# A convolution, selective-scan and attention kernel: the head by lines with two PSUM tiles in turn, the first delta kept in SBUF, four lanes for the last stage

## The chip, the cores and the metric

The kernel runs on one core of one Trainium2 chip. The metric is the device time of one execution in microseconds (us); smaller is better. Times are medians of several executions, and every run counted here is of the fast state or, where a kernel ran only once, of a state that can't be told. Two executions of the same kernel easily differ by 10 us (26 runs of the kernel before lay between 5500.35 and 5524.82), so single microseconds are read from the profiles, as far as they repeat (see e0 to e2), and the times say whether they arrive at the end.

## The reference, cut to what matters

Four images of 64 x 64 pixels and 96 channels pass one convolution block with a selective scan in four directions, then linear attention and a small feed-forward net.

```python
# per image: L = 4096 pixels, Dn = 192 channels, N = 16 states, K = 4 directions
xz = bilinear(groupnorm(x), W_in)            # products of signs
xp, z = split(xz)
t = conv3x3(sign(xp + move0), sc * sign(conv_W)) + biases
t = prelu(t) + xp
u = t * sigmoid(t)                           # silu
xs = [u by rows, u by columns, both backwards]
dts, B, C = bilinear(xs, Wl)                 # again products of signs
delta = softplus(bilinear(dts, Wd) + bias)
h = exp(delta * A) * h + (delta * u) * B     # the scan along the 4096 pixels
y = sum_over_states(h * C) + D * u
out = layernorm(sum of the 4 directions) * silu(z) @ W_out   # then + x
t = t + linear_attention(layernorm(t)); t = t + ffn(layernorm(t))
```

The names in the profile follow this: `cv` is the convolution's result in PSUM, `v` and `r` are the two branches of prelu, `u` the block's result and `ut` the same by columns, `xg` and `sg` its signs, `xr` the signs transposed, `tbc` the rows of B and C, `gT` the signs that delta is made from, `dl` delta and delta * u spread over the 16 states, `bc` B and C spread over the channels.

## The kernel before

The scan is cut into 1536 pieces of 128 x 1024. For each piece GpSimd makes the input w = (delta u) * B, ScalarE the decay, VectorE the scan, and the product with C goes to VectorE or GpSimd, whichever a running tally of costs finds less loaded:

```python
lead = c.vec.us - c.gps.us
c.vec.us, c.gps.us = max(0.0, min(lead, 8.0)), max(0.0, min(-lead, 8.0))
pool = c.vec.us + 1.2 > c.gps.us + 2.4          # the product goes to GpSimd
h = c.p.h.tile([128, CH], F32, ...) if pool else dA
c.vec.tensor_tensor_scan(h, dA, w, first, ALU.mult, ALU.add)
```

The head (image 0 alone, nothing of the scans beside it) loads small weights early, makes the convolution part by part in the two halves of one PSUM tile, and starts the scans by way of memory:

```python
for g in range(NG):                              # 24 loads of 2 KB each
    ...
        nc.sync.dma_start(anm[j::4, g, :], src[j])
...
two = [c.p.dA.tile([128, CH], F32, ...) for i in range(2)] if alone else None
parts = [(h, q) for h in range(2) for q in range(NQ8)]
for n, part in enumerate(parts + [None]):
    at = 512 * (n % 2)
    ps = two[0][:, at : at + 512]                # 15 groups of matmuls into ps
    ...
    nc.vector.tensor_scalar(v, ps, ...)
    nc.scalar.activation(r, ps, AF.Relu, ...)
...
def run(self, back):
    ...                                          # three parts of delta, stored to dld
    c.later.flush()
    self.load_dl(0)                              # and loaded again, spread over the states
    for m in (1, 2):
        self.load_dl(m)
    ...                                          # a fourth part before the loop
    self.decay(0)
    for i in range(AHEAD):
        self.inject(i)                           # w of the first four pieces, GpSimd
    for i in range(n): ...                       # loop: inject(i + 4), product of i - 1, scan(i)
```

The tail is the last image's layer norms ("sums"), one small step ("middle") and the last stage ("last"), in three lanes that step in turn:

```python
e.alone = True
more = [e.spare_lane(x) for x in range(2)]
drain([behind] + [e.sums(ln) for ln in more])
drain([e.middle()])
drain([e.last(ln) for ln in [e.lane] + more])
```

## Time and profile before

| kernel before | |
|---|---|
| median of the first 3 runs | 5511.64 us (5508.68 to 5516.53) |
| span of the profiled execution (its time 5505.96 us) | 5504.2 us |
| convolution starts | 71.2 us |
| last u | 192.7 us |
| gT complete | 231.1 us |
| GpSimd's first product for the scans | 260.93 us |
| last product of the scans ends | 5388.80 us |
| from there to the end | 115.4 us |

The times inside are read from the list of instructions of the profiled execution, counted from its start. The profiled execution was one of the quick ones of its kernel; a second profile of the same head (e2) has the last u 5 us earlier. The lines of the profile that carry the argument stand in the prediction.

### The profile page before, as it was taken

What the parts mean: (1) busy time and instruction counts of PE and PEld (TensorE: products, weight loads), DVE (VectorE), ACT (ScalarE), POOL (GpSimd) and SP (SyncE); (2) the same over time, 40 slices, a digit from 0 to 9 for tenths busy, and PEclk for the clock granted to TensorE, in tenths of its full rate; (3) what the DMA queues carried; (4) which work ended last, traced back from release to release, by engine and by line L of the source; (5) the groups of instructions that cost most, each with busy time, mean ns of one, the idle gap of its engine ahead of it and who ended that gap; (6) DMA issues with size and microseconds to landing.
All of it is one profiled execution on the core that took longest, in us unless ns stands there. A gap on an engine that the chain in (4) does not pass through costs nothing. (4 is left out here: it accounts for less than half of the span.)

```text
span 5504.2 us, 62064 instructions
## 1 busy us (share of the span) xinstructions
PE 3466.0 (63%) x20089; PEld 1360.3 (25%) x20089; DVE 4996.1 (91%) x3142; ACT 3631.0 (66%) x5673; POOL 4947.3 (90%) x2247
## 2 busy tenths in 40 slices
PE   5456765467655776656665677664777664444677
PEld 2221222122222232222222222221232221111223
DVE  3299999999999999999999999999999999999884
ACT  4468776677766667777767666775656775655544
POOL 2199999899999999999999999999999999999981
PEclk7666876578867777768876787766787665556777
DMA  4455665766666666676765666666666565765642
GB/s 78 122 184 195 206 203 188 245 214 208 209 200 202 195 205 211 201 235 212 219 192 185 207 211 195 205 217 225 198 209 203 178 198 196 219 204 185 203 152 60
DMA packets 613659, 1069.84 MB, mean 194 GB/s; under 512 B 225147, under 2 KB 344468, under 8 KB 611540
## 3 DMA queue, kind: packets, MB, share of 16 engines
q1 hardware_dynamic: 612244, 1065.86, 61.3%
q8 instruction: 157, 2.57, 0.2%
q14 instruction: 170, 1.39, 0.1%
q10 hardware_dynamic: 1088, 0.02, 0.0%
HBM read 833.16 MB, written 229.35 MB: 193 GB/s over the span
## 5 line engine op out<-in xcount | busy, mean ns | idle before, releaser
L421 POOL TENSOR_TENSOR w<-dl,bc 128x1024 f32<-128x1024 f32 x1536 | 3580.9, 2358 | 155.5 <-PE yp L1409 72.6
L1336 ACT ACTIVATE dA<-dl,anm 128x1024 f32<-128x1024 f32 x1536 | 1714.5, 1116 | 474.4 <-DVE w L421 285.8
L421 DVE TENSOR_TENSOR_SCAN dA<-dA,cy,w 128x1024 f32<-128x1024 f32 x726 | 1700.9, 2343 | 90.7 <-ACT dA L1336 75.5
L1409 PE MATMUL yp<-w,sum 128*32 128x256 f32 x12288 | 1286.6, 514 | 384.8 <-POOL w L421 230.7
L421 POOL TENSOR_TENSOR w<-h,bc 128x1024 f32<-128x1024 f32 x573 | 1349.1, 2355 | 124.1 <-DVE h L421 110.0
L421 DVE TENSOR_TENSOR w<-dA,bc 128x1024 f32<-128x1024 f32 x963 | 1179.5, 1225 | 54.7 <-DVE dA L421 0.5
L421 DVE TENSOR_TENSOR_SCAN h<-dA,cy,w 128x1024 f32<-128x1024 f32 x426 | 996.7, 2340 | 16.0 <-ACT dA L1336 15.8
L1409 PEld LDWEIGHTS yp<-w,sum 128*32 128x32 f32 x12288 | 315.6, 128 | 1467.9 <-issue 690.1
L1378 ACT COPY cy<-dA 128x1 f32<-128x1 f32 x721 | 113.5, 157 | 772.5 <-DVE w L421 770.6
L421 DVE TENSOR_TENSOR_SCAN dA<-dA,w 128x1024 f32<-128x1024 f32 x237 | 540.9, 2282 | 36.7 <-ACT dA L1336 28.4
L1271 PE MATMUL dps<-gT,wdz 128*128 128x64 fp8e5 x1000 | 113.9, 313 | 358.8 <-ACT ys L1423 329.8
L421 DVE TENSOR_TENSOR_SCAN h<-dA,w 128x1024 f32<-128x1024 f32 x147 | 334.8, 2278 | 4.9 <-ACT dA L1336 3.4
L1284 PE MATMUL dps<-sp,ident 128*128 128x512 f32 x376 | 273.0, 815 | 46.0 <-ACT dps L1280 45.8
L1414 PE MATMUL yp<-ya,back 128*128 128x256 f32 x576 | 235.1, 528 | 4.5 <-DMA ya<-yd 2.5
L659 PE MATMUL cv<-tp,cwA 128*96 128x512 fp8e5 x576 | 198.4, 470 | 60.3 <-ACT r L706 55.1
L1271 PEld LDWEIGHTS <-wdz 128*128 128x128 fp8e5 x1024 | 95.4, 152 | 440.1 <-issue 409.7
L1271 PE MATMUL dps<-gT,wdy 128*128 128x64 fp8e5 x504 | 58.5, 317 | 205.2 <-ACT ys L1423 203.2
L1276 ACT ACTIVATE pd<-dps,dbias,pvd 128x512 f32<-128x512 f32 x188 | 143.3, 762 | 20.2 <-PE dps L1271 20.2
L1414 PEld LDWEIGHTS yp<-ya,back 128*128 128x128 f32 x576 | 122.6, 246 | 133.4 <-issue 93.5
L1378 ACT COPY cy<-h 128x1 f32<-128x1 f32 x431 | 79.9, 185 | 113.7 <-DVE h L421 112.8
L941 PE MATMUL yc<-eys,mean 96*96 96x512 f32 x240 | 132.1, 702 | 24.2 <-DVE vks L421 8.9
L1277 ACT ACTIVATE sp<-dps,dbias,pvd 128x512 f32<-128x512 f32 x188 | 144.2, 767 | 0.0
(312 smaller groups left out, 4433.1 us busy)
## 6 DMA issues: line engine op xcount, KB each, us to landing
dl<-dld SPq DMA_DIRECT2D x768, 512.0 KB
bc<-bcd SPq DMA_DIRECT2D x512, 512.0 KB
dld<-pd SPq DMA_DIRECT2D x125, 512.0 KB
yd<-ys SPq DMA_DIRECT2D x768, 64.0 KB
dld<-pd SPq DMA_DIRECT2D x126, 256.0 KB
ya<-yd SPq DMA_DIRECT2D x192, 128.0 KB
pu<-ud SPq DMA_DIRECT2D x32, 512.0 KB
pu<-utd SPq DMA_DIRECT2D x30, 512.0 KB
```

What stands on the lines that cost most here:

```text
L421: return getattr(self.eng, name)(out, *args, **kw)
L659: nc.tensor.matmul(ps, w[:, 96 * h : 96 * h + 96], tp[:, 8 * q + dy : 8 * q + dy + 8, dx : dx + IW], start=(w is taps[0][1]), stop=(w is t ...
L941: self.c.nc.tensor.matmul(ps, w, x, start=(i == 0), stop=(i == len(pairs) - 1))
L1271: nc.tensor.matmul(pv[:, s], wd[:, k, s], gT[:, :, c0 : c0 + 16], start=(s == 0), stop=(s == 7))
L1276: nc.scalar.activation(d[:, 0], ps, AF.Abs, scale=sc, bias=bi)
L1277: nc.scalar.activation(t, ps, AF.Relu, scale=sc, bias=bi)
L1284: nc.tensor.matmul(ps, c.ident, t, start=False, stop=True, skip_group_check=True)
L1336: c.nc.scalar.activation(t, self.dlt[i // NQ][0], AF.Exp, scale=c.anm[:, g, NQ * KORD[e] + q : NQ * KORD[e] + q + 1])
L1378: self.c.nc.scalar.copy(self.carries[g, q], h[:, CH - 1 : CH])
L1409: c.nc.tensor.matmul(y[32 * x : 32 * x + 32, g % 2, :], c.sum4, prod[:, 256 * x : 256 * x + 256], start=(q == 0), stop=(q == NQ - 1 and no ...
L1414: c.nc.tensor.matmul(y[:, g % 2, :], w, src, start=False, stop=(n == len(more) - 1))
```

## The change

Its intent is to shorten what isn't scans. It loads the small weights last, alternates two PSUM tiles in the convolution and goes through it by lines (both halves of the channels of a line, then the next line), stores signs in larger pieces, makes the first delta out of SBUF and spreads it from SBUF to SBUF, and at the end uses four lanes and loads the short operands first. Cut to its core:

```diff
-        (early)  sbR and anm loads
+        (after all weights)
+        for k in range(NK):  nc.sync.dma_start(sbR[...], ...)            # 12 issues
+        for g in range(NG):  ... nc.sync.dma_start(anm[j::4, g, :], ...) # 24 issues
@@ projections
-                px, pz = two[1][:, 0:512], two[1][0:96, 512:CH]
+                px, pz = (c.p.ps.tile([128, 512], F32, ..., tag=f"y{j}") for j, x in enumerate("xz"))
-                sz = c.p.h.tile([128, CH], F32, ...)           # stored for each q
+                    if q % 4 == 0:
+                        szs[h] = c.p.w.tile([128, CH], F32, ...)  # stored for four q at once
@@ convolution
+                parts = [(h, q) for q in range(NQ8) for h in range(2)]
-                    ps = (two[0][:, at : at + 512] if alone else bank("cv" + nm, 0))[0:96]
+                        ps = c.p.dA.tile([128, CH], F32, name=f"cv{nm}_{b}", tag="dA")[0:96, 0:512]
+                per = 2 if alone and h else 4                   # u by columns: six stores for four
@@ transposes
+            xrs = rw.tile([128, 96, 64], BF16, ...)             # first in its pool
-                        nc.scalar.copy(prev[0], prev[1])
+                        (nc.vector.tensor_copy if fast and n % 2 else nc.scalar.copy)(prev[0], prev[1])
@@ scans
-        pool = c.vec.us + 1.2 > c.gps.us + 2.4
+        pool = c.vec.us + 1.2 > c.gps.us + 2.4 and i < len(self.pieces) - 2
+    def start(self):                                            # two parts of delta, then
+        for n in range(3):
+            for x in range(2):
+                r = p.dl.tile([128, CH], F32, ...)
+                nc.sync.dma_start(r, w[x][32 * n : 32 * n + 32].unsqueeze(1).to_broadcast([32, 4, CH]))
+            if n == 0:
+                for q in range(NQ):
+                    self.load_bc(1, self.ct, 0, 0, 0, q)
@@ tail
+    more.append(e.fourth_lane())                                # between middle and sums
-                self.loads(ln, q, ("ys", "sz", "xb"))
+                self.loads(ln, q, ("sz", "xb", "ys") if self.alone else ("ys", "sz", "xb"))
-        c.gps.tensor_tensor(m0, self.vks, c.hmask, ALU.mult)
+        (c.vec if self.alone else c.gps).tensor_tensor(m0, self.vks, c.hmask, ALU.mult)
```

## The prediction

> **What bounds the kernel now.** I read the page first: the span, the busy shares, the forty slices.
>
> ```profile
> span 5504.2 us, 62064 instructions
> PE 3466.0 (63%) x20089; PEld 1360.3 (25%) x20089; DVE 4996.1 (91%) x3142; ACT 3631.0 (66%) x5673; POOL 4947.3 (90%) x2247
> DVE  3299999999999999999999999999999999999884
> POOL 2199999899999999999999999999999999999981
> ```
>
> VectorE and GpSimd are both full from the third slice to the last but one. Then I cut the span with the stage table at the first scan work (GpSimd's first product starts at 260.9 us) and at the last product (5388.8 us).
>
> ```profile
> core 0: us, PE busy (x) PEld busy (x) DVE busy (x) ACT busy (x) POOL busy (x), PEclk, DMA share, GB/s
> 275.00:5389.00 5114.00, 3245.84 (x19162) 1246.97 (x19165) 4867.19 (x2907) 3446.53 (x5370) 4889.09 (x2130) 0.72 0.63 202
> ```
>
> In those 5114 us each of the two is busy 95%, and the diff alters two of the 1536 pieces there. So the change can only shorten the head (261 us) and the tail (5504 - 5389 = 115 us). All 376 us would have to shrink by 110 us to reach 2%. What the head waits for, from the waits of 56 to 200 us and of 203 to 280 us:
>
> ```profile
> PE cv L659 <- ACT r L706: 33.3, 15, 3.7
> POOL ut L634 <- DMA utd<-ut: 25.2, 3, 8.5
> ACT r L706 <- DVE v L703: 21.2, 11, 2.9
> ACT sz L600 <- DMA szd<-sz: 12.2, 1, 12.2
> ...
> POOL w L421 <- DMA dl<-dld: 57.8, 1, 57.8
> DVE w_s L421 <- DMA pu_s<-utd: 22.3, 1, 22.3
> ACT xr L740 <- DMA utd<-ut: 10.2, 1, 10.2
> ```
>
> First number: us in total. Line 1: each convolution part's matmuls wait until ScalarE has read the part before, though they go to the other half of the tile. Line 4: one stop of 12.2 us before the convolution. Its cause is in SyncE's timeline: the store of sz stands behind 18 us of issues for anm.
>
> ```profile
> 43.03 18.07 SPq L269 DMA_DIRECT2D anm<-in_al  x24
> 61.21 4.49 SPq L440 DMA_DIRECT2D xbd<-xb  x8
> 65.80 14.37 SPq L440 DMA_DIRECT2D szd<-sz  x6
> ```
>
> **What the Trainium skill says.** (1) "PSUM — Partial Sum Buffer", section "PSUM bank collisions raise a hardware error": two engines may not touch one bank and quadrant at once, reads included, and the compiler orders them. The trace agrees: r (ScalarE) and v (VectorE) only read the same tile, yet r starts 0.83 us after v, in 11 waits. (2) "DMA: Bandwidth & Descriptors", "Rules for kernel authors": a strided last dimension becomes one descriptor per element. The trace agrees: an anm load of 2 KB holds SyncE for 18.07 / 24 = 0.75 us. (3) Same page, "Anatomy of one DMA": about 2.0 us fixed per transfer. The trace has more in queues: 7.0 us from the first dl issue (253.90) to GpSimd's start (260.93). (4) "GPSIMD Engine Reference", "Elementwise — side-by-side cycle accounting": float32 tensor_tensor is 1.96 times slower there than on VectorE. Here 2355 against 1225 ns, 1.92.
>
> **The change part by part.**
>
> *Up to the convolution (starts 71.2 us now).* The new yield puts the column sums ahead of the w_in signs. Now the sums start at 18.60, behind ScalarE's twelve sbR issues and those signs; x is issued by 4.6 us, so they can run from about 5 to 13 us. The next barrier is older: VectorE reads cw_n until 25.6 us, since the loads land then; xb, now on VectorE, queues behind that, and GpSimd's sign copies follow. So the chain is ahead by some 4.5 us at 33 us (copies begin at 29 in place of 33.8), not by 13. Without the stop of 12.2 us the convolution would now begin near 58.5. Minus 4.5 gives 54. Against it: the projections move to banks y0 and y1, which the weights' transposes use, so casts (1.22 us) and signs (1.5 to 2.3 us) alternate with the matmuls; five such rounds at some 0.5 us each: start 56, a gain of **15**.
>
> *The convolution.* Two tiles end the wait of line 1, but another loop is hidden right behind it: v 0.84, r 0.82, second combination 0.8, sign 0.6, exponential 0.6, logarithm and exponential 1.3, u 0.7, then v again: 5.65 us, exactly the distance of parts that run undisturbed (v at 138.80 and 144.44). v and r still share a bank. Only the four parts that came 1.0 to 1.25 us late behind TensorE gain: about **5** with part 0. The twelve projections are the same ScalarE work, one per part in place of two: nothing. But anm (18 us) and sbR (twelve issues of about 0.4, some 5 us) now come in at the second part, in front of u's and sg's stores; v of part n reuses the buffer of sg of part n-2, sg that of u of part n-2. SyncE blocks from about 9 to 32 us after the start, part 2's sg was due at 22 and can run at 33: a loss of **12**. The by-columns stores become six in place of four, each holding the queue 6 us (the 6.03 after a utd issue), twice two in a row: a loss of **3**. In sum the convolution costs 10 more; its last u, now at 192.7, comes at about 187.7.
>
> *Transposes.* xr now lies first in its pool, so it no longer waits for the by-columns store (10.1 us from the last u to its first copy). In the place of that wait: the last sg store goes out behind the store of half 0, which blocks 6.6 us; the transposes can start some 6.9 us after the last u. Gain **3**. Copies on two engines: 12 groups now take 7.2 us on ScalarE (0.58 each and waits), TensorE needs 0.53 per group: gain **1**. The scaling of tbc by VectorE: tbc and sgn read the same bank, so matmul 1.07, tbc 0.85, sgn 0.8 per tile, two tiles in turn, is 1.4 us per tile against 1.34 now: **0**. Up to the signs gT (231.1 now): 5 + 3 + 1 = 9, so 222.
>
> *The first delta.* Now from gT to GpSimd's first product 260.9 - 231.1 = 29.8 us, with a store to memory, loads behind 4 MB of bc, and then the first scan held to 271.1 by a fourth part whose u load stands behind the dl loads. New: matmuls until +2.1, eight activations of two parts 5.2 us, the last two VectorE pairs until +9.5 (the float32 matmuls of 0.87 us go, an add of 0.69 comes), then the broadcast out of SBUF, which I put at the same 7.0: +16.5. GpSimd gains **13.3**; VectorE, which starts after one product, about 21. As the two are equally full, I count **15** at the end of the scans.
>
> *Tail.* Last two products: now both scans end 5386.3 and GpSimd's two products (2.35 each) end 5388.8. On VectorE from 5381.7: scan 2.25, product 1.22, twice, is 5388.7: **0**. Loads with sz and xb ahead of ys: these 384 KB go in front of the one transfer that is awaited: a loss of **0.7**. hmask on VectorE: gain 0.2. Four lanes:
>
> ```profile
> 5432.75:5457.94 25.19, 20.63 (x69) 9.16 (x70) 12.23 (x24) 14.47 (x24) 0.00 (x0) 0.71 0.15 43
> 5457.94:5482.07 24.13, 19.02 (x74) 8.79 (x73) 14.16 (x27) 14.43 (x24) 0.00 (x0) 0.86 0.15 42
> 5482.07:5504.20 22.13, 13.51 (x48) 6.11 (x47) 10.03 (x19) 9.81 (x16) 0.00 (x0) 0.79 0.13 36
> ```
>
> Eight pieces go in rounds of 3, 3 and 2. The second takes 24.1 us, the third 18.2 up to its last matmul (5500.3): 6 us per lane, 6 fixed. Two rounds of four: 2 x 30.3 = 60.6, against 25.2 + 24.1 + 18.2 = 67.5. The fourth lane's first load is the tenth in the queue instead of none, lane three's was the seventh and was waited for: minus 2. Gain **5**.
>
> *Sum.* Head 9 + 15 = 24, tail 4.5: 28.5 us. The two starting states of the scans may add a little, so I say 5511.6 - 30.6 = **5481 us**, 0.56% less.
>
> **The rivals.** (a) *The small loads don't block.* If anm's and sbR's issues fall where nothing waits, the 12 us come back and the time is about 5469. For it: they were put last on purpose. Against it: buffers turn over in 1.6 parts, 9 us, and 23 us of issues are in one piece. (b) *The head's gain is lost in the scans.* GpSimd starts earlier, VectorE earlier still, and the first products meet ct loads and the remaining delta lanes, now three steps per piece; if the pair runs dry, only 5 to 10 of the 15 us stay: about 5490. For it: two engines at 95% in step have little slack. Against it: dl and bc land at 300 to 400 GB/s there. (c) *TensorE was the real bound of the convolution* and v and r overlap: 16 x 0.8 us more, 5468. Against it are the undisturbed 5.65 us. (d) *Nothing in the head counts, since the scan chain alone decides*: 5505; spoken against by the engines' idleness before 261 us.
>
> **Range and chances.** My errors are the stop in the convolution (0 to 15), the start (8 to 21), the weights (5 to 20 for what I call 15), and about 4 us from run to run (5508.7 to 5516.5). They don't all fall on one side: 5462 to 5499. Faster by over 2% needs 5401 us, more than the whole head could plausibly give: 0.01. Slower by 2% would need a broken scan loop: 0.005.
>
> **What would show it.** Right: the convolution starts at 52 to 60 us with no szd wait before it; its matmuls no longer wait for r but v and r keep 0.83 us apart and parts 5.65; one stop of about 12 us near part 2, with SyncE in anm; xr's copies wait for TensorE and not for utd; GpSimd's first product near 237; the scans end about 24 us earlier; the tail, from the last product on, is 111 in place of 115 us; two rounds of about 30 us. Wrong: parts below 5.3 us, no stop behind anm, a first product later than 245, or a GpSimd share between first and last product below 95%. A time below 5460 would say that I invented a stall; one above 5500 that the scans give the head's gain back.

## The result, and the profile after

The changed kernel takes **5496.23 us** (median of 4 runs, 5494.50 to 5501.43) against 5512.47 (4 runs, 5508.68 to 5516.53). The ratio is 0.9972, with a 95% interval of 0.9955 to 0.9989. (A ratio is the mean time of one kernel's fast runs over that of the other's of the same rounds, so it isn't quite the ratio of the medians.) The gain is 15 us, a second measurement below gives 18; the prediction said 30.6. The result is correct.

The page of the changed kernel:

```profile
span 5492.7 us, 62021 instructions
...
PE 3452.2 (63%) x20083; PEld 1352.5 (25%) x20083; DVE 5015.4 (91%) x3170; ACT 3614.5 (66%) x5648; POOL 4940.8 (90%) x2246
...
DVE  4499999999999999999999999999999999999985
...
POOL 2399999899999999999999999999999999999980
```

In the second slice (137 to 275 us) VectorE rose from 2 to 4 tenths and GpSimd from 1 to 3: the scans start earlier. The stage table of the scans:

```profile
core 0: us, PE busy (x) PEld busy (x) DVE busy (x) ACT busy (x) POOL busy (x), PEclk, DMA share, GB/s
250.00:5377.00 5127.00, 3237.32 (x19158) 1243.32 (x19162) 4868.57 (x2908) 3443.73 (x5366) 4885.80 (x2134) 0.72 0.63 202
```

VectorE and GpSimd are busy 95% there, as before. In both profiles I read the same marks; differences are after minus before.

| mark | before, us | after, us | difference | predicted |
|---|---|---|---|---|
| convolution starts | 71.2 | 56.1 | -15.1 | -15 |
| last u | 192.7 | 176.1 | -16.7 | -5 |
| gT complete | 231.1 | 216.7 | -14.4 | -9 |
| GpSimd's first product | 260.9 | 235.7 | -25.2 | -24 |
| first scan | 271.2 | 238.1 | -33.1 | -30 (9 + 21) |
| fourth scan | 279.3 | 259.1 | -20.2 | counted as -24 |
| last product to end | 115.4 | 115.9 | +0.5 | -4.5 |

The lead that the first product has (25 us) is 20 four scans later, and the tail gave nothing in this pair of profiles. The waits of the changed kernel between 60 and 177 us (total, times, longest) answer to those of the convolution in the prediction:

```profile
POOL ut L655 <- DVE u L423: 104.4, 15, 23.2
DVE u L423 <- ACT e L713: 54.5, 15, 4.6
ACT r L729 <- DVE v L726: 29.8, 16, 4.3
```

The wait of the convolution's matmuls for r (33.3 us before) has left the list, and so has the stop of sz. That ScalarE waits for v stays: in each of the 16 parts r starts 0.83 or 0.84 us after v. SyncE's timeline shows that the small loads really stand in the convolution now (start, duration):

```profile
76.22 16.25 SPq L392 DMA_DIRECT2D anm<-in_al  x24
92.56 0.57 SPq L442 DMA_DIRECT2D ud<-u  x1
93.23 1.84 SPq L442 DMA_DIRECT2D xg<-sg  x3
```

But no part is late by them: v of the first seven parts follow each other at 12.1, 6.8, 7.7, 6.8, 7.7 and 6.8 us, and those distances belong to the projections, which end with the twelfth part (then 5.6 to 6.0). Behind gT, between 188 and 260 us, two waits matter:

```profile
DVE h L423 <- POOL w L423: 19.5, 3, 9.9
...
ACT xr L765 <- DMA utd<-ut: 12.4, 1, 12.4
```

The wait of xr for the store of ut, which the change was to end, is still there. And a new one: VectorE's early scans wait for GpSimd, 9.9 us in one piece.

### The profile page after: what moved, and what is told of

It reads as the page before. It is cut to its first block, busy times and chain, and to the rows that moved or that the text cites. A ratio compares the mean times of both kernels' runs of the same rounds, so it can differ in the third digit from the quotient of the medians.

```text
span 5492.7 us, 62021 instructions
## 1 busy us (share of the span) xinstructions
PE 3452.2 (63%) x20083; PEld 1352.5 (25%) x20083; DVE 5015.4 (91%) x3170; ACT 3614.5 (66%) x5648; POOL 4940.8 (90%) x2246
## 5 line engine op out<-in xcount | busy, mean ns | idle before, releaser
L423 POOL TENSOR_TENSOR w<-dl,bc 128x1024 f32<-128x1024 f32 x1524 | 3550.6, 2356 | 103.4 <-PE yp L1462 77.3
L423 DVE TENSOR_TENSOR w<-dA,bc 128x1024 f32<-128x1024 f32 x965 | 1181.9, 1225 | 55.0 <-DVE dA L423 0.5
L1329 ACT ACTIVATE pd<-dps,dbias,pvd 128x512 f32<-128x512 f32 x189 | 143.8, 761 | 19.7 <-PE dps L1324 13.5
```

The costliest lines, as they stand in the source:

```text
L423: return getattr(self.eng, name)(out, *args, **kw)
L1329: nc.scalar.activation(d[:, 0], ps, AF.Abs, scale=sc, bias=bi)
```

## The experiments

The experiments ran in three groups of four (e0 to e3, e4 to e7, and the rest). The kernels of a group shared one chip with runs of the kernel before, and the groups had different chips. So across groups I compare ratios to the kernel before; 0.0010 is 5.5 us.

### Does the loop give the gain back? (e0, e1, e2)

Set beside each other, the first two profiles say so: at the last scan the lead is only 10.8 us. The two kernels place 584 of the 1536 C products on different engines, since the tally starts from other values. e0 is the changed kernel once more. e1 and e2 exchange the placements:

```diff
+PLACES = "..."      # 1536 digits: the other kernel's choice for each product
-        pool = c.vec.us + 1.2 > c.gps.us + 2.4 ...
+        pool = PLACES[i] == "1"
```

> The changed kernel once more, unaltered, to see how much of its scan loop is the same from run to run, and as the partner of the next two on the same chip. In its first profile scan number 30 starts 19 us earlier than before the change, scan number 1000 only 4 us, the last one 11 us. If that loss is in the program, this profile shows the same stretches (320 to 415: a loss of 9 us; 928 to 991: a loss of 9, then 5 back). If it is chance, the losses lie elsewhere. Time: 5493 to 5502 us.

> The changed kernel, but for every piece the C product goes to the engine on which it went before the change (a list of 1536 bits in place of the tally's own choice; the last two stay on VectorE). Theory 1 (the head's lead is lost because the tally, started from another state, puts some 12 of every 32 products on the other engine, in places that suit the loop less): the lead of about 20 us at scan 30 stays to the end within 3 us, time 5484 to 5489. Rival (the scan loop takes its pace from something that an earlier start doesn't move, or from where its transfers fall in time): the lead goes down to 8 to 12 us as in the changed kernel, time 5494 to 5502.

> The kernel before, with the changed kernel's places of the C products (the last two products stay as they were). Theory 1: the loop gets 5 to 10 us longer, 5517 to 5523. Rival: unchanged within 3 us, 5509 to 5515.

Measured: e0 5493.08 us (6 runs, ratio 0.9967, interval 0.9955 to 0.9978). e1 5494.06 (5 runs, 0.9964, 0.9951 to 0.9976). e2 5513.70 (21 runs, 1.0004, 0.9997 to 1.0011), the kernel before beside them 5513.54 (26 runs). In the times my theory **fell**: e1 isn't clear of e0, and e2 lies 2 us above its kernel (-2 to +6), where I expected 5 to 10 more. The profiles of e0 and e1 differ (spans 5497.4 and 5484.1), but e1's profiled execution was the quickest of its five, and that of the kernel before was quick too.

By stretches, as e0's expectation asks, the profiles do show the placement. The lead is how much earlier a scan (counted from 0) starts than in the first profile of the kernel before:

| C products placed | profiles | lead lost, scan 320 to 415, us | lost, 928 to 991, us | lost, scan 30 to the last, us |
|---|---|---|---|---|
| as in the changed kernel | after, e0, e2, e3, e4, e6, e9, e10 | 8.7 to 10.4 | 6.0 to 7.4 | 3 to 14 |
| as before | e1, e5 | 1.7, 1.2 | 0.4, 1.5 | 3, 10 |

So the two losses repeat and go with the placement; they are not chance. From scan 991 on the first group gets 4 to 11 us back, and over the whole loop the groups overlap: what the placement costs in total is not shown. Over the first 30 scans it costs 4 us: with the same head, e1 is 3.7 us ahead of the changed kernel at scan 30.

Where do profiles repeat? Those of the changed kernel to about a microsecond up to the signs (gT at 215.9 to 217.1 us in after, e0, e1, e3, e4, e5, e7), and to 2.4 us after the last product. Those of the kernel before do not: in e2, whose program is the same up to the scans, the convolution's v take 102.8 us from first to last and not 107.0, gT is complete at 225.9 us and not 231.1, and the tail takes 118.1 us and not 115.4. So a difference to the kernel before has some 5 us of play in the head and 3 in the tail. From here on I mostly compare the changed kernel with its own variants, and leave the total to the times.

### Order of the loads at the end (e3)

```diff
-                self.loads(ln, q, ("sz", "xb", "ys") if self.alone else ("ys", "sz", "xb"))
+                self.loads(ln, q, ("ys", "sz", "xb"))
```

> The changed kernel with one order undone: in the last stage ys is loaded ahead of sz and xb again. Read from the profile, not from the time. In the changed kernel the first mean matmul starts 11.7 us after the last product (5376.8 to 5388.5), before the change 9.5 us (5388.8 to 5398.35). If the two small loads in front of ys cost this, it is 9.5 us again, and the tail from the last product on is 2 us shorter, 114 in place of 116. If the wait comes from elsewhere (the queue, the clock), it stays 11 to 12.

One run, 5488.22 us. In its profile the first mean of the tail starts 9.72 us after the last product, against 11.71 in the changed kernel and 9.52 before. So the new order costs 2.0 us, where I had put 0.7: ys is what the first matmul awaits, and two short loads for each lane now stand ahead of it. (The seven other profiles with the new tail have 11.67 to 12.50.)

### The whole tail undone (e4)

```diff
-    more.append(e.fourth_lane())
-                self.loads(ln, q, ("sz", "xb", "ys") if self.alone else ("ys", "sz", "xb"))
+                self.loads(ln, q, ("ys", "sz", "xb"))
-        (c.vec if self.alone else c.gps).tensor_tensor(m0, ...)
+        c.gps.tensor_tensor(m0, ...)
-        pool = ... and i < len(self.pieces) - 2
+        pool = ...
```

> The changed kernel with the whole tail of before put back: three lanes, ys loaded first, hmask's product on GpSimd, the last two products placed by the tally. Theory from the profiles: the change's tail is worth nothing (115.9 us from the last product to the end in the changed kernel, 115.4 in the one before), because what four lanes save in the middle part (4.8 us) is spent on the fourth lane's loads (3.2) and on the order of loads (2.1). Then this runs as the changed kernel does, 5494 us, with a tail of about 115.4 us in its profile. The prediction's step says that the tail is worth 4.5 us: then 5498 to 5499 us and a tail of 119 to 120 us. In the pieces of the tail: last product to first mean 9.5, mean to middle 30.4, middle to the last part 5.0, last part to end 70.4 us.

Measured: 5495.82 us (9 runs, ratio 0.9973, 0.9964 to 0.9983), against 0.9972 and 0.9967 of the changed kernel. By these ratios all the work on the tail is worth 0.5 to 3 us, not 4.5, though their intervals (5 us and more to each side) don't decide it. Its parts, in us, from the traces:

| | last product to first mean | to the middle's result | to the last stage's first norm | to the end | sum |
|---|---|---|---|---|---|
| before | 9.52 | 30.44 | 4.96 | 70.45 | 115.4 |
| e2 (tail of before) | 9.67 | 33.49 | 4.90 | 70.09 | 118.1 |
| after | 11.71 | 31.12 | 7.37 | 65.72 | 115.9 |
| e0 (after again) | 11.77 | 30.70 | 8.16 | 65.27 | 115.9 |
| e3 | 9.72 | 30.79 | 8.07 | 66.62 | 115.2 |
| e4 | 9.94 | 30.52 | 5.34 | 71.89 | 117.7 |

The three profiles with the old tail (before, e2, e4) take 117.1 us on average, the eight with the new one (114.1 to 116.5) 115.7: a gain of 1.4, where the first pair shows a loss of 0.5. Four lanes do save 5 us in the last column and give 2.4 to 3.2 back in the third; the order of the loads takes 2 in the first. The third column is a queue. SyncE's issues at the start of the last stage in the changed kernel:

```profile
5415.94 0.30 SPq L1161 DMA_DIRECT2D tt<-td  x1
5416.33 0.38 SPq L1166 DMA_DIRECT2D x1b<-x1d  x1
5416.81 0.36 SPq L1161 DMA_DIRECT2D tt<-td  x1
...
5418.62 0.43 SPq L1161 DMA_DIRECT2D ln1d<-td  x1
...
5420.03 0.42 SPq L1161 DMA_DIRECT2D l4t<-td  x1
```

Each lane asks for its operand, its residual and its next operand before the next lane asks for anything. The fourth lane's first operand leaves 4.1 us after the first lane's, and the lanes step in turn, so all four wait for it.

### The first delta by way of memory (e5)

```diff
-        for _ in self.start():
-            pass
+        (run() of before up to self.decay(0): three parts stored to dld,
+         loaded by load_dl, the fourth part before the loop)
-            for _ in range(3 if i < 3 else 1):
-                interleave(lanes)
+            interleave(lanes)
```

> The changed kernel with the start of the scans of before: the first delta is stored to memory and loaded again, four parts before the loop. It measures what the first delta from SBUF is worth at the end. The prediction counted 15 us: then 5509 us. Theory from the profiles: GpSimd's first product comes 10.8 us later here, but with the changed start 2.5 us of that are lost again to two waits for delta lanes and VectorE stands at its third scan until GpSimd has made six injections, so that only 6 to 9 us are left at the fourth scan: 5500 to 5503 us. Expected in its profile: gT at about 217 us as in the changed kernel, the first GpSimd product at about 246.5, the fourth scan at 265 to 268 (259.1 in the changed kernel).

Measured: 5500.07 us (15 runs, ratio 0.9978, 0.9970 to 0.9985), so 3 to 6 us slower than the changed kernel by the ratios, whose intervals overlap. The first product of GpSimd comes at 244.9 us (changed kernel 235.7), the first scan at 254.7 (238.1), but the fourth scan at 263.3 (259.1). So 9.2 us at the first product, 4.2 at the fourth scan, some 5 in the time.

Two things differ there, though: e5's tally also places every product but the last two as before. With the placement held equal, the first delta is worth more. Counted from gT, scan 30 comes 8.1 us later in e5 than in e1, and 8.8 later in e2 than in the changed kernel; the ratios of e5 and e1 (0.9978, 0.9964) differ by 8 us (their intervals just overlap). So the first delta from SBUF, for which the prediction counted 15 us, is worth 8 to 9, and the placement that came with it takes some 4 of them.

### u by columns in idle tiles (e6)

xr doesn't lie on ut's memory, yet in the built program its first copies wait for the semaphores of ut's stores. (In e6 xr lies at the same address, and they no longer do.) The pool of ut is closed just before the pool of xr is opened, and the framework lets the first write wait for all that used the closed pool.

```diff
-                    uts[h] = utp.tile([96, IW, 8 * per], F32, ...)
+                    t = c.p.bc.tile([128, CH], F32, ..., tag=f"bc{h}")[0:96]   # per = 2 for both h
+                    uts[h] = t.rearrange("p (w h) -> p w h", h=16)
```

> The changed kernel with the tiles of u by columns taken from idle tiles of the scans, 16 rows each, and no pool of their own that closes ahead of xr. Theory: xr's first copy waits in the changed kernel for the last store of ut (at 188.4 us) although the first transposes are done at 182.3, only because the framework makes everything in the next pool wait for what used the closed one. Then the copies start at about 182.5 us, 6 us earlier, gT comes about 6 us earlier (211), and the time is 5488 us. Rival: the last store of ut is awaited by something else as well (the first u load, sgn, gT's chain) so that gT comes less than 2 us earlier and the time stays at 5494. The two more stores of 6 us each can also delay u's stores: then the last u comes later than 176.1.

Measured: 5488.26 us (5 runs, ratio 0.9958, 0.9945 to 0.9970), 5 to 8 us faster than the changed kernel by the ratios; the intervals overlap, but the profile shows it too. The waits between 170 and 200 us:

```profile
PE xa L764 <- DMA xg<-sg: 15.4, 1, 15.4
...
ACT xr L769 <- PE xa L764: 8.7, 4, 6.3
DVE xr L769 <- PE xa L764: 7.1, 4, 5.1
```

xr's copies now wait for TensorE, as the prediction had wanted it, and start at 182.61 us instead of 188.36. From there the gain is handed on whole to gT, at 211.0 (216.7), and the first product, at 229.8 (235.7); at the fourth scan it is 4.7 us (254.4 against 259.1). The copies themselves take no less than before: 8.0 us from the first to the end of the twelfth, against 7.5 before and 8.1 in the changed kernel. Two engines in turn gave nothing.

### The first four products on VectorE (e7)

```diff
-        pool = c.vec.us + 1.2 > c.gps.us + 2.4 and i < len(self.pieces) - 2
+        pool = c.vec.us + 1.2 > c.gps.us + 2.4 and 4 <= i < len(self.pieces) - 2
```

> The changed kernel with the first four products of C forced onto VectorE. Theory: at the start of the scans GpSimd is the one that is behind (six injections before it can make product 0) and VectorE idles 12 to 16 us in the first 30 us, 9.9 of them in one wait at the third scan; products moved to VectorE fill idle time and take 2.35 us each off GpSimd. Then the fourth scan starts 6 us or more ahead of the changed kernel's (259.1), and the time falls by 3 to 6 us to about 5489 to 5491. Rival (the scans are level and only the sum of work counts): 4 products moved are 4 x 2.35 less for one and 4 x 1.22 more for the other, and the tally then gives them back within the next pieces: no change, 5494 us.

Measured: 5486.74 us (5 runs, ratio 0.9956, 0.9943 to 0.9968), 6 to 9 us faster than the changed kernel by the ratios; again the intervals overlap. The timelines show why. First the changed kernel, VectorE and then GpSimd (start, duration, what; in brackets the idle time before it and what ended it):

```profile
238.07 4.59 DVE L423 TENSOR_TENSOR_SCAN h<-dA,w 128x1024 f32<-128x1024 f32 x2 [5.96 <-POOL w L423]
242.58 0.67 DVE L423 TENSOR_TENSOR pd<-dps,pu 128x512 f32<-128x512 f32 x1
253.14 2.29 DVE L423 TENSOR_TENSOR_SCAN h<-dA,w 128x1024 f32<-128x1024 f32 x1 [9.90 <-POOL w L423]
259.10 2.29 DVE L423 TENSOR_TENSOR_SCAN h<-dA,w 128x1024 f32<-128x1024 f32 x1 [3.67 <-POOL w L423]
```

```profile
235.69 9.26 POOL L423 TENSOR_TENSOR w<-dl_s,bc 128x1024 f32<-128x1024 f32 x4 [47.09 <-DMA bc<-bcd]
246.18 4.63 POOL L423 TENSOR_TENSOR w<-dl_s,bc 128x1024 f32<-128x1024 f32 x2 [1.23 <-DMA dl_s<-w_s]
250.77 2.34 POOL L423 TENSOR_TENSOR w<-h,bc 128x1024 f32<-128x1024 f32 x1
254.43 2.34 POOL L423 TENSOR_TENSOR w<-dl_s,bc 128x1024 f32<-128x1024 f32 x1 [1.31 <-DMA dld<-w_s]
```

The first products of C (`w<-h`) are GpSimd's, but six inputs (`w<-dl_s`) stand ahead of them in its order, and there are two tiles for h. The third scan needs the tile of the first, so VectorE, after two scans, waits until GpSimd has done six inputs and a product. In e7 the same stretch of VectorE reads:

```profile
238.01 2.30 DVE L423 TENSOR_TENSOR_SCAN dA<-dA,w 128x1024 f32<-128x1024 f32 x1 [6.73 <-POOL w L423]
240.34 1.23 DVE L423 TENSOR_TENSOR w<-dA,bc 128x1024 f32<-128x1024 f32 x1
241.48 2.29 DVE L423 TENSOR_TENSOR_SCAN dA<-dA,w 128x1024 f32<-128x1024 f32 x1
...
249.01 2.29 DVE L423 TENSOR_TENSOR_SCAN dA<-dA,w 128x1024 f32<-128x1024 f32 x1
```

The fourth scan comes at 249.0 us instead of 259.1. The seventh waits 5.9 us for GpSimd again, and at scan 30 the gain is 5.7 us (341.0 against 346.7). The tally places the later products differently too, so the time alone doesn't show the cause. Why the tally had chosen otherwise can be read off it when the program is built: before the first scan it stands at 36.9 us for VectorE and 11.8 for GpSimd. VectorE's sum is work of the convolution and the first delta, done long ago. The clamp leaves 8 us of it, and these send the first four products to the engine that is behind.

### Everything that helped, and the same with three lanes (e8, e11)

e8 takes e6, the first six products on VectorE, ys first, and two more reorderings; e11 is e8 without the line `more.append(e.fourth_lane())`.

```diff
@@ start()
-            if n == 0:
-                for q in range(NQ):
-                    self.load_bc(1, self.ct, 0, 0, 0, q)
+            for q in range(2 * n, min(2 * n + 2, NQ)):
+                self.load_bc(1, self.ct, 0, 0, 0, q)
@@ last()
         nxt = fetch(n)
+        if self.alone:
+            yield                       # every lane's first operand goes out first
         x1 = residual(nxt[0]) if nxt else None
```

> The changed kernel with everything that helped: u by columns in idle tiles, the first six products of C on VectorE, ys loaded first at the end, the second pair of delta lanes loaded between the second and third tile of C at the start, and in the last part each lane's first operand loaded before any lane's second one. If the gains add: 6 (idle tiles) + 6.4 (first products) + 2.1 (order of loads) + 1 to 3 (delta pair, last part) = 15 to 17 us below the changed kernel's 5494, that is 5477 to 5480 us. Rival: gains of the start overlap (the first products only filled idle time that the earlier gT takes away too) and the time stays at 5482 to 5486.

> As e8_best, with three lanes in place of four for the last stage. If four lanes are worth what the prediction put on them (5 us), this has 5 us more from the last product to the end; if the fourth lane's loads eat it (theory), 0 to 2 us more.

Measured: e8 **5485.16 us** (6 runs, 5474.69 to 5489.84; ratio 0.9948, 0.9934 to 0.9962), e11 5487.68 (5 runs; 0.9957, 0.9942 to 0.9972). e8 beats the kernel before by 0.5%. Against the changed kernel it never ran on the same chip; the ratios 0.9948 and 0.9967 to 0.9972 put it about 12 us ahead.

The tail is now clear: from the last product to the end e8 takes 109.7 us and e11 115.4 in their profiles. **Four lanes are worth 5.7 us** once the loads are in the right order (one profile of each; the times differ by 5, within their intervals), quite what the prediction put on them. The last stage's issues in e8:

```profile
5406.08 0.30 SPq L1165 DMA_DIRECT2D tt<-td  x1
5406.48 0.37 SPq L1165 DMA_DIRECT2D ln0d<-td  x1
5406.90 0.42 SPq L1165 DMA_DIRECT2D ln1d<-td  x1
5407.37 0.42 SPq L1165 DMA_DIRECT2D l4t<-td  x1
```

The fourth lane's operand leaves 1.3 us after the first lane's, not 4.1, and the stretch up to the first norm falls from 7.4 to 4.8 us.

In its scans e8 came out below what I expected. Its fourth scan is 36.3 us ahead of the kernel before (20.2 in the changed kernel), at scan 320 it is 33.2, and e11 has 35.9 and 32.9. But of e8's gain in time, 0.0052 of some 5512 us or 29 us, 5.7 are the tail, and 23 are left for the scans; e11's 24 us are all scans. So some 10 us of the longest leads are lost in the loop, though the intervals of these gains are 8 us to each side. In the profiles most of it goes between scans 320 and 415 (6.8 us in e8, 6.2 in e11) and between 600 and 928 (7.4 and 5.3); both kernels have a placement of their own, and why it goes there I can't say.

### One tile for the convolution (e9)

```diff
+            one_cv = c.p.dA.tile([128, CH], F32, name=f"cv_{b}", tag="dA") if alone else None
-                        ps = c.p.dA.tile([128, CH], F32, name=f"cv{nm}_{b}", tag="dA")[0:96, 0:512]
+                        at = 512 * (n % 2)
+                        ps = one_cv[:, at : at + 512][0:96]
```

> The changed kernel with one two-bank tile for the convolution in place of two in turn, as before. It is read from the profile: from the first v to the last. The prediction put two tiles at 5 us of gain, by four parts that were 1.0 to 1.25 us late; the changed kernel takes 107.8 us for the fifteen distances (7.2 us each), and the kernel before 107.0. If the prediction's mechanism holds, this takes about 113 us and the first product of GpSimd comes 5 us later (241); if the loop behind it (v, r, combination, sign, exponential, u, 5.6 us) and the projections set the distance anyway, 108 to 109. If TensorE were the bound it would be 120 or more.

One run, 5505.83 us. The first v to the last takes 112.6 us (107.8 in the changed kernel), the last u comes at 181.5 (176.1), the first product at 241.3 (235.7). The wait is back, here in the waits between 60 and 182 us:

```profile
PE cv L684 <- ACT r L731: 35.4, 14, 3.7
```

So two tiles save 4.9 us from the first v to the last and 5.4 at the last u, against 5 predicted, and by the predicted mechanism. Two more things follow. A wait of 35 us in total was worth only 5, since it lay beside the loop of v, r, sign and u. And with one tile, the new order by lines takes 112.6 us where the old one took 107.0 (102.8 in e2). The distances from v to v point to the projections: one beside each of twelve parts (the first 12.1 us, then 6.8 to 8.6 here) takes more than two beside each of six (7.4 to 9.6 before). I had put that at nothing; no run tests it alone.

### The small loads early again (e10)

```diff
+        (sbR's loads on ScalarE, anm's on SyncE, before the weights, as in the kernel before)
-        (the same loads after the weights)
```

> The changed kernel with the small loads of anm and sbR issued where the kernel before has them, early on SyncE and ScalarE. The prediction says that they caused the stop of 12.2 us before the convolution, and that where they are now they stop its second part for 12 us (which the profile of the changed kernel doesn't show). If the first is right, the convolution starts 8 to 14 us later here (64 to 70 us instead of 56.1). Rival: the stop went because sz now has two large tiles of its own and no store has to be awaited; then the convolution starts within 3 us of 56 and the move of the small loads was worth little.

One run, 5501.18 us. The convolution starts at 59.2 us, 3.1 later than in the changed kernel, not 8 to 14. SyncE, in the profile of e10:

```profile
44.20 17.57 SPq L269 DMA_DIRECT2D anm<-in_al  x24
61.88 2.51 SPq L441 DMA_DIRECT2D xbd<-xb  x5
```

It is held for 17.6 us at the same place as before, and no wait of sz for a store is left: sz now has tiles of its own. So moving the loads is worth 3.1 of the 15.1 us, and the stop of 12.2 us, which the prediction put down to anm, went with the other changes before the convolution, most likely sz's own tiles (no run undoes them alone). And from the first v to the last this takes 107.4 us; with the loads inside the convolution it is 107.5 to 107.9 (seven profiles). They cost 0.1 to 0.5 us there, hardly more than the scatter, not 12.

## Why the prediction was wrong

It said 5481 us, and 5496 came: the direction was right, the value lay inside the range, but of the 30.6 us about 15 to 18 came. Its first step already missed something: "the diff alters two of the 1536 pieces there". The tally starts from other values, and 584 products change their engine. Step by step, with what stands in the prediction first:

| step | predicted gain, us | measured, us | by |
|---|---|---|---|
| up to the convolution | 15 | 15.1 | profile; partly luck, the cause was another (e10) |
| two tiles | 5 | 5.4 | e9 |
| small loads inside the convolution | -12 | -0.4 | e10 |
| stores by columns, projections | -3 | -3.4 | rest of the stage |
| transposes up to gT | 3 + 1 | -2.3 | profile, e6 |
| the first delta, at the end of the scans | 15 | 5.8, placement included (8 to 9 without) | fourth scan; e5 with e1 |
| tail | 4.5 | -0.5 (1.4 by all profiles) | profile, e4 |
| two starting states | 2.1 | not seen | |

The third to fifth lines follow from the marks: convolution start to last u takes 121.5 us before and 119.9 after (gain 1.6 = 5.4 - 0.4 - 3.4), and last u to gT 38.4 and 40.7. The first delta is what the fourth scan has more than gT, 20.2 - 14.4. The measured column adds up to 19.7 us, of which 15 to 18 arrive. It holds for the first pair of profiles: set against e2, the stores and projections cost 4.4 us more, and the fourth scan's lead is 17.0 us, not 20.2. That so much was left is partly luck: the convolution was predicted to lose 10 us and gained 1.6 (against e2 it lost 2.8), which hid a first delta 9 us and transposes 6 us short of their forecast.

**The step that failed most is the first delta: "As the two are equally full, I count 15 at the end of the scans."** Its matmuls and activations were right (the first spread is issued 9.2 us after gT, 9.5 predicted for the end of the two parts). The spread out of SBUF took 9.8 us from issue to the first product and not 7.0, so GpSimd gained 10.9 us and not 13.3. (What came last there is the last tile of B in one profile and the spread in another.) And then "the two are equally full" doesn't hold at the start. VectorE's lead of 33 us at the first scan is of no use, because scans three and four wait for GpSimd (9.9 and 3.7 us). GpSimd stands still twice: 1.2 us for the second pair of deltas, which is issued behind the four tiles of C, and 1.3 us more. e5 and e1 show what remains, 8 to 9 us with the placement held equal and some 5 with the one that came with it, and e7 that the place of the first products was at fault: with four of them on the idle engine the fourth scan is 10 us earlier and scan 30 still 5.7. Rival (b) had this ("if the pair runs dry, only 5 to 10 of the 15 us stay"), with 5490 us; it was the better bet.

**The tail** failed in its small terms, not in its large one. Four lanes are worth 5.7 us (e8 against e11), but the order of the loads costs 2.0 and not 0.7 (e3), and the fourth lane's first load 2.4 to 3.2 and not 2; together they ate most of the gain.

**The transposes**: "xr now lies first in its pool, so it no longer waits" was wrong. I looked at memory, and the wait hangs on the closing of a pool. It cost 5.7 us (e6).

**The convolution** erred the other way. "SyncE blocks from about 9 to 32 us after the start ... a loss of 12" took the eight buffers of v, u, sg and their like for a ring. In the built program v of the third part sits in the buffer of the first part's sg, whose store went out at 67.99 us, ahead of the block (69.93 to 92.5), and the fourth part's v in that of the third's. So the stores behind the block were of buffers that hardly anyone needed yet (sg waits 1.9 us in all for stores of u). Rival (a), the small loads don't block, was right about the mechanism and wrong about the time, as other steps failed. Rival (c), TensorE as the bound of the convolution, is refuted: v and r keep 0.83 us apart. Rival (d) is refuted by every ratio.

What stays open: why the changed kernel's placement loses 9 to 10 us between scans 320 and 415, and what it costs in total; and why leads of 33 us at scan 30 shrink by some 10 us in the loop (e8, e11), while 24 and 25 us arrive nearly whole (e6, e7).

## What to carry to other kernels

When two full engines take turns, an earlier start of one is worth only what the slower start of the other leaves: read the first few pieces one by one, and look at what the load balancer believes before the first of them. Its starting value can move work all through the program (584 of 1536 products here), so hold the placement equal when you measure something else. Profile both kernels twice before you trust a difference of 5 us. When you add a lane, look at the issue order of its first load before you count its gain; and ask of each wait on a buffer whether it hangs on memory or on the closing of a pool. A wait that leads a list (here 35 us) may be worth 5, if another loop of nearly the same length lies behind it.

## What the Trainium skill lacked or had wrong

- No page has it that tiles of a newly opened pool can wait for the stores of a pool just closed though their memory doesn't overlap: xr's first copies came 5.7 us later for it (188.36 against 182.61 us in e6). Nor does any say that a pool's buffers need not come round in turn, which made 12 us of a predicted stop into 0.5 at most.
- "PSUM — Partial Sum Buffer", section "PSUM bank collisions raise a hardware error", agrees (v and r of one bank start 0.83 us apart in all 16 parts of the changed kernel). It gives no measure of what alternating two tiles is worth: here 4.9 to 5.4 us of a listed wait of 35.4.
- "DMA: Bandwidth & Descriptors", section "Rules for kernel authors", warns of one descriptor per element, and the runs agree (anm: 24 loads of 512 numbers, 12288 in all, fall in a stretch with 13072 packets below 512 B, and hold SyncE for 16.25 us). It doesn't say when this is free: in e10 17.57 us of it delayed the convolution by only 3.1 us.
- The same page, section "Anatomy of one DMA", gives a fixed cost of about 2.0 us, but for transfers that GpSimd issues; those here are issued by SyncE, and the prediction's use of the figure is cut. For a pair of spreads from SBUF to SBUF in a busy queue the page has no number: here it was 9.8 us from the first issue (225.93) to GpSimd's start (235.69), with 2 MB of other loads issued just before it.
- "GPSIMD Engine Reference", section "Elementwise — side-by-side cycle accounting", agrees: its 1.96 for float32 stands against 2356 / 1225 ns = 1.92 in the changed kernel.
